# Four tiles of int8 transposes moved behind the last gate product, and two layernorm steps fused

## The chip, the cores and the metric

The kernel runs on one core of a Trainium2 chip. A core has five engines with queues of their own: TensorE (PE: matrix products and transposes, results into PSUM), VectorE (DVE), ScalarE (ACT), GpSimd (POOL) and SyncE (SP, which only issues DMAs here). The weight loads of TensorE are shown apart as PEld. The metric is the device time of one execution in microseconds; lower is better. The kernel before took 1231.49 us, the median of three runs (1229.37 to 1232.19).

## The reference, cut to what matters

One input of 625 nodes by 1024 features goes through four residual layers, each on a layernorm of what came before:

```python
x = x + gated_rgcn(_layernorm(x))     # 8 relations, then tanh(u) * z + x * (1 - z), z = [u, x] @ w_gate
x = x + int8_linear(_layernorm(x))    # one scale for the whole tensor
x = x + gcn(_layernorm(x))            # x @ W.T + b, then a sum over neighbours with symmetric norms
x = x + moe(_layernorm(x))            # top-2 of 8 experts, and a shared expert

def _layernorm(x, axis=-1, eps=1e-05):
    m = jnp.mean(x, axis=axis, keepdims=True)
    v = jnp.var(x, axis=axis, keepdims=True)
    return (x - m) / jnp.sqrt(v + eps)

# int8_linear
x_scale = jnp.maximum(jnp.abs(x2).max() / 127.0, EPS)
x_int8 = jnp.clip(jnp.round(x2 / x_scale), -128, 127).astype(jnp.int8)
acc_i32 = jax.lax.dot_general(x_int8, weight_int8.T, ..., preferred_element_type=jnp.int32)
out = acc_i32.astype(jnp.float32) * x_scale * weight_scale.T + bias
```

What matters here is the step from the first layer to the second. The int8 scale is one number for all 625 rows, so no element can be quantised before the last row has been gated and normalised.

## The kernel before, in words

The 625 nodes are five tiles of 125 rows (`NT` is 5, `P` is 125). A tile `X[t]` holds rows on partitions and 1024 features along them. TensorE contracts over partitions, so an operand that is multiplied by a weight is first transposed into `xT`, which holds eight blocks of 128 features by 625 nodes.

The first layer's relation products (L429, L649) fill the kernel up to about 836 us. Then comes the stage that the change touches:

- `gate(t, h)` (L772) multiplies `xT` of tile `t` by half `h` of the gate weights: eight products of 512 columns (sixteen records in the profile, since each is run as two). VectorE then finishes the gate with three steps on 512 columns (L785 to L787) and so completes half of `X[t]`.
- After both halves of a tile, `layernorm` (L172) normalises `X[t]` into `th[t]`, and L841 takes the largest magnitude of each row into a column of `am`.
- `transposed` (L177) turns `th[t]` back into `xT`. It works in two groups of four transposes. Each group fills one PSUM buffer of `ps_tr`, which has two, and ScalarE copies the buffer into `xT` (L186). A third group therefore waits for the first group's copy.
- `btot` holds the adjacency counts of all relations, five rows of blocks. Its transpose `aT` is made at L855 from five transposes for each row of blocks, in two PSUM buffers of the same pool (four blocks in one, the fifth in the other), and copied by ScalarE at L858. It is used only much later, at L959.
- `am1` (L863) is the largest magnitude of each partition. TensorE spreads it over all partitions (the product named amT, L865), and VectorE makes the scale and its inverse (L867 to L870).
- `quantize(t)` (L880) scales, rounds and clips `xT` of one tile in three VectorE steps into `qT`. Tile 0 is done in two halves. `quantized(t)` (L903) multiplies it by the int8 weights, held in bf16 (L908, sixteen products for a tile), and VectorE adds the result to `X[t]` and normalises it again. `columns(t)` (L925) transposes that and multiplies by the weights of the third layer (L931). The order of the two is written out at L948.

`layernorm` calls `ln_stats` (L156), which takes mean and variance, and `rsqrt` (L144): ScalarE takes the square root, VectorE the reciprocal, and one Newton step refines it. It is called with one value for a row (125x1) by every layernorm, and with five (125x5) once, for the degrees. Twenty layernorms run: five at the start, five after the gates, five after the int8 products, five after the third layer.

Three things set the order of the instructions. `on_pe` and `tc.issue_after(pe_last.ins)` chain steps on TensorE: a step may not be issued ahead of the one before it in the chain. `behind` does the same between two single instructions. Within those bounds the framework's planner orders each engine's queue by its own estimates when the kernel is built. The queue is then fixed, and each engine runs its own in that order. The adjacency transposes and tile 4's transposes (L850 to L859) are issued after `pe_last`, but `pe_last` is not advanced by them: only the amT product (L865) becomes the next `pe_last`.

## Time and profile before

| | |
|---|---|
| median of three runs | 1231.49 us |
| profiled execution, its own time | 1231.8 us |
| its span | 1230.0 us |
| mean granted TensorE clock | 0.987 |
| TensorE busy | 1192.4 us, 97% |
| VectorE busy | 846.7 us, 69% |
| ScalarE busy | 172.2 us, 14% |
| relation products (L429) on the chain | 48% |
| gate products (L777) on the chain | 6% |
| int8 products (L908) on the chain | 18 us (1.5%) |

The profile gives start and duration of each instruction, and in brackets the engine's idle time before it with what ended it. The chain of waits follows the work that ended last back through what released each step. A line such as "PE mm L908 x48" is 48 records of line 908 on TensorE. A stretch gives each engine's busy time between two moments, then the clock granted to TensorE (1.00 is full), the share of DMA that was busy and the GB/s moved.

### The profile page before, as it was taken

What the parts mean: (1) busy time and instruction counts of PE and PEld (TensorE: products, weight loads), DVE (VectorE), ACT (ScalarE), POOL (GpSimd) and SP (SyncE); (2) the same over time, 40 slices, a digit from 0 to 9 for tenths busy, and PEclk for the clock granted to TensorE, in tenths of its full rate; (3) what the DMA queues carried; (4) which work ended last, traced back from release to release, by engine and by line L of the source; (5) the groups of instructions that cost most, each with busy time, mean ns of one, the idle gap of its engine ahead of it and who ended that gap; (6) DMA issues with size and microseconds to landing.
All of it is one profiled execution on the core that took longest, in us unless ns stands there. A gap on an engine that the chain in (4) does not pass through costs nothing.

```text
span 1230.0 us, 11161 instructions
## 1 busy us (share of the span) xinstructions
PE 1192.4 (97%) x3850; PEld 653.6 (53%) x3850; DVE 846.7 (69%) x1360; ACT 172.2 (14%) x308; POOL 487.2 (40%) x227
## 2 busy tenths in 40 slices
PE   5999999999999999999999999999999999999996
PEld 2444444444444444444437888885445447766663
DVE  6879888888888888883336888865979516471111
ACT  1100000000000000000021212213321111213331
POOL 1005787888787888987700000003310000023322
PEclk9999999999999999999999999999999999999998
DMA  9995836373737373626175679606340016279973
GB/s 265 268 255 129 211 64 202 62 203 62 203 63 202 65 201 65 180 43 180 1 182 143 176 185 270 174 1 161 102 137 17 17 35 200 82 236 264 281 159 55
DMA packets 155984, 178.36 MB, mean 145 GB/s; under 512 B 78469, under 2 KB 95228, under 8 KB 155920
## 3 DMA queue, kind: packets, MB, share of 16 engines
q1 hardware_dynamic: 66082, 132.28, 37.0%
q0 software_dynamic: 72992, 13.31, 10.7%
q10 hardware_dynamic: 16846, 31.98, 8.5%
q8 instruction: 32, 0.52, 0.2%
q14 instruction: 32, 0.26, 0.1%
HBM read 131.66 MB, written 45.50 MB: 144 GB/s over the span
## 4 chain that ended last, share of the span: by engine, by line
PE 91%; DMA 4%; ACT 2%; DVE 1%; issue 1%; POOL 0%; SPq 0%; ACTq 0%; POOLq 0%; DVEq 0%
PE mm L429 48%; PE mm L649 14%; PE mm L777 6%; PE mm L931 6%; PE mm L1357 4%; PE mm L1330 3%; PE mm L959 2%; DMA w<-in_L_gnn_weight_dram 2%; PE tr L183 2%; PE mm L1259 2%; PE mm L908 1%; PE mm L1045 1%; DMA y<-yd 1%; PE lgT L1032 1%; ACT xT L186 1%
## 5 line engine op out<-in xcount | busy, mean ns | idle before, releaser
L387 POOL DMA_INDIRECT table<-hits,idx x165 | 408.1, 2474 | 198.7 <-DVE idx L383 99.3
L429 PE MATMUL mm<-w,xT 128*125 128x512 f32 x800 | 350.8, 593 | 0.2 <-DMA w<-in_L_gnn_weight_dram 0.2
L363 DVE SCALAR_TENSOR_TENSOR junk<-kr,key,wm 125x1375 f32<-125x1375 f32 x165 | 271.7, 1646 | 1.1
L429 PEld LDWEIGHTS mm<-w,xT 128*125 128x125 f32 x800 | 150.1, 188 | 192.3 <-issue 188.6
L649 PE MATMUL mm<-y,b 125*125 125x512 f32 x400 | 160.7, 402 | 2.3 <-issue 1.4
L649 PE MATMUL mm<-hi,b 125*125 125x512 f32 x400 | 159.1, 398 | 0.0
L429 PE MATMUL mm<-t,btot 128*125 128x512 f32 x320 | 143.8, 592 | 0.0
L1314 POOL DMA_INDIRECT th<-tokens,token_i x16 | 17.4, 1086 | 214.5 <-DVE token_i L1198 174.4
L429 PEld LDWEIGHTS mm<-t,btot 128*125 128x125 f32 x320 | 60.1, 188 | 77.3 <-issue 77.3
L981 POOL IOTA io<- 125x40 f32 x1 | 0.2, 207 | 227.8 <-ACT th L762 227.8
L649 PEld LDWEIGHTS mm<-y,b 125*125 125x125 f32 x400 | 75.0, 187 | 23.6 <-DVE y L614 3.4
L712 DVE SCALAR_TENSOR_TENSOR X<-mm,rc,X 125x512 f32<-125x512 f32 x80 | 60.0, 751 | 38.8 <-PE mm L649 38.0
L649 PEld LDWEIGHTS mm<-hi,b 125*125 125x125 f32 x400 | 75.1, 188 | 18.2
L429 PE MATMUL mm<-t,xT 128*125 128x512 f32 x160 | 71.9, 592 | 0.0
L429 PE MATMUL mm<-w,btot 128*125 128x512 f32 x160 | 71.9, 592 | 0.0
L931 PE MATMUL mm<-w,xT 128*125 128x512 f32 x160 | 70.0, 595 | 1.6 <-ACT xT L186 1.6
L777 PE MATMUL mm<-w,xT 128*125 128x512 f32 x160 | 71.0, 604 | 0.0
L609 ACT CAST hi<-y 125x512 fp32r<-125x512 f32 x80 | 43.3, 617 | 148.3 <-PE mm L649 131.3
L1357 PE MATMUL mm<-w,th 128*98 128x512 f32 x128 | 56.3, 592 | 0.0
L614 DVE TENSOR_TENSOR y<-y,hi 125x512 fp32r<-125x512 f32 x80 | 53.6, 681 | 0.0
L448 ACT COPY y<-mm 125x512 f32<-125x512 f32 x18 | 10.5, 586 | 302.5 <-PE mm L429 291.7
L422 DVE TENSOR_TENSOR t<-w,t 128x2048 f32<-128x2048 f32 x20 | 45.8, 2290 | 8.1 <-DMA w<-in_L_gnn_weight_dram 7.6
(220 smaller groups left out, 1170.4 us busy)
## 6 DMA issues: line engine op xcount, KB each, us to landing
w<-in_L_gnn_weight_dram SPq DMA_DIRECT2D x32, 1024.0 KB
w<-in_L_ffn_w_dram SPq DMA_DIRECT2D x16, 1024.0 KB
yd<-y ACTq DMA_DIRECT2D x70, 224.0 KB
y<-yd SPq DMA_DIRECT2D x70, 224.0 KB
table<-zero SPq DMA_DIRECT2D x4, 3054.0 KB
b<-table SPq DMA_DIRECT2D x8, 1367.2 KB
kr<-key_rows ACTq DMA_DIRECT2D x15, 601.6 KB
w<-in_L_gnn_w_gate_dram SPq DMA_DIRECT2D x8, 1024.0 KB
```

The source lines that it names most:

```text
L363: d = nc.vector.scalar_tensor_tensor(junk, kr, key[:, c : c + 1], wm[:, (EG - 1 - j) * P : (2 * EG - 1 - j) * P], op0=ALU.is_equal, op1=AL ...
L387: d = nc.gpsimd.indirect_dma_start(out=table, out_offset=bass.IndirectOffsetOnAxis(ap=idx[:, c : c + 1], axis=0), in_=hits[:, c : c + 1], ...
L422: d = nc.vector.tensor_sub(o, v, w)
L429: last = nc.tensor.matmul(ps[:P, :], lhs[:, k], rhs[:, k], start=(start and k == 0), stop=(stop and k == 3))
L609: upper.append(nc.scalar.copy(hi, y))
L614: turns.append(nc.vector.tensor_sub(lo, y, hi.bitcast(F32)))
L649: last = nc.tensor.matmul(ps[:P, :], counted[r][:, k, t * P : (t + 1) * P], part, start=(k == ks[0] and part is parts[r, h, k][0]), stop=( ...
L712: nc.vector.scalar_tensor_tensor(X[at][:, hs], v[:P, :], rc[:, r, at : at + 1], X[at][:, hs], op0=ALU.mult, op1=ALU.add,)
L777: last = nc.tensor.matmul(ps[:P, :], xT[:, 4 * i + k, t * P : (t + 1) * P], gate_w[h][i][:, k, :], start=(i == 0 and k == 0), stop=(i == 1 ...
L931: last = nc.tensor.matmul(ps[:P, :], xT[:, k, t * P : (t + 1) * P], gcn_w[h][k // 4][:, k % 4, :], start=(k == 0), stop=(k == KD - 1),)
L1330: last = nc.tensor.matmul(ps[:, :CAP], weights[e][0][:, k, f * 128 : (f + 1) * 128], tiles["xeT"][e % 2][:, k, :], start=(k == 0), stop=(k ...
L1357: last = nc.tensor.matmul(ps[:CP, :], he[:, f, j * CP : (j + 1) * CP], weights[e][1][:, f, hs], start=(f == 0), stop=(f == 1),)
```

## The change

Two things are changed.

First, the int8 transposes. Before, tile 0's transposes stood between the two gate halves of tile 3, and tile 1's between those of tile 4; those of tiles 2 and 3 stood behind the last gate product. Now those of tiles 0 to 3 all stand behind the last gate product, one tile after the other. Tile 4's stay where they were in the text, after the adjacency rows.

Second, the layernorm. For one value a row, two multiplications of the Newton step become one instruction that multiplies twice; the shape with five values keeps the two. The copy of the mean now stands behind the addition of epsilon to the variance instead of ahead of it.

```diff
@@ rsqrt
         t = small.tile(shape, F32, tag="rq_t", name="rq_t")
-        nc.vector.tensor_mul(t, v, y0)
-        nc.vector.tensor_mul(t, t, y0)
+        if shape[1] == 1:
+            nc.vector.scalar_tensor_tensor(t, v, y0, y0, op0=ALU.mult, op1=ALU.mult)
+        else:
+            nc.vector.tensor_mul(t, v, y0)
+            nc.vector.tensor_mul(t, t, y0)
         nc.vector.tensor_scalar(t, t, -0.5, 1.5, op0=ALU.mult, op1=ALU.add)
@@ ln_stats
         nc.vector.bn_aggr(mv, st.rearrange("p a b -> p (a b)"))
-        nc.vector.tensor_copy(mean_rstd[:, 0:1], mv[:, 0:1])
         ve = small.tile([P, 1], F32, tag="ln_ve", name="ln_ve")
         nc.vector.tensor_scalar_add(ve, mv[:, 1:2], EPS)
+        nc.vector.tensor_copy(mean_rstd[:, 0:1], mv[:, 0:1])
         rsqrt(mean_rstd[:, 1:2], ve, [P, 1])
@@ the gate loop
             with tc.issue_after(pe_last.ins):
                 pe_last, added = gate(t, h)
-            if h == 0 and t >= 3:
-                on_pe(transposed, xT, (t - 3) * P, th[t - 3], P)
             if t > 0:
@@ behind the gate loop
-    for t in (NT - 3, NT - 2):
+    for t in range(NT - 1):
         on_pe(transposed, xT, t * P, th[t], P)
```

## The prediction

> **What bounds the kernel now.** I read the page first, for the bound; then the chain in order of time around the changed steps; then TensorE's timeline there, VectorE's timeline, and stretches of one clock state each.

> ```profile
> PE 1192.4 (97%) x3850; PEld 653.6 (53%) x3850; DVE 846.7 (69%) x1360; ACT 172.2 (14%) x308; POOL 487.2 (40%) x227
> PEclk9999999999999999999999999999999999999998
> PE 91%; DMA 4%; ACT 2%; DVE 1%; issue 1%; POOL 0%; SPq 0%; ACTq 0%; POOLq 0%; DVEq 0%
> ```

> TensorE is the bound, busy 97% and 91% of the chain, so a step counts only if it moves TensorE's next dense product. The chain shows where TensorE is not dense:

> ```profile
> 907.47 6.87 PE mm L777 x16
> 914.34 0.44 PE tr L183 x4
> 914.80 0.59 ACT xT L186
> 915.44 0.66 PE tr L183 x4
> ...
> 924.50 1.93 PE tr L183 x8
> 926.43 11.11 PE mm L908 x48
> 937.53 0.44 PE tr L183 x4
> ```

> Last gate product, then twelve microseconds in which each transpose waits for ScalarE's copy out of PSUM, then the int8 products (L908). TensorE's timeline there:

> ```profile
> 916.75 0.85 PE L855 MATMUL tr<-ident,btot 125*125 125x125 f32 x5 [0.19 <-ACT xT L186]
> 918.12 0.81 PE L855 MATMUL tr<-ident,btot 125*125 125x125 f32 x5 [0.51 <-ACT aT L858]
> 920.85 1.32 PE L855 MATMUL tr<-ident,btot 125*125 125x125 f32 x5 [0.56 <-ACT aT L858]
> 922.62 1.41 PE L855 MATMUL tr<-ident,btot 125*125 125x125 f32 x5 [0.25 <-ACT aT L858]
> 926.22 11.31 PE L908 MATMUL mm<-w,btot 128*125 128x512 bf16 x48
> ```

> A row of the adjacency matrix (five transposes) takes 1.36 us, later 1.8 us. The stretches say why (second PE share, granted clock before the DMA share):

> ```profile
> 914.17:917.58 3.41, 2.98 (x22) 2.28 (x20) 3.03 (x6) 2.21 (x5) 0.00 (x0) 1.00 0.97 302
> 917.58:920.99 3.41, 1.78 (x12) 1.38 (x12) 2.74 (x9) 2.22 (x7) 0.00 (x0) 1.00 0.38 147
> 920.99:924.40 3.41, 2.80 (x11) 2.12 (x11) 2.21 (x9) 1.27 (x4) 0.00 (x0) 0.50 0.00 0
> 924.40:927.82 3.42, 3.32 (x12) 2.65 (x13) 3.28 (x7) 1.37 (x4) 0.00 (x0) 0.50 0.02 5
> ```

> The granted clock is halved from 920.99 to 927.82, into the first products. VectorE meanwhile:

> ```profile
> 914.38 0.69 DVE L785 TENSOR_TENSOR z<-mm,gx 125x512 f32<-125x512 f32 x1 [4.05 <-PE mm L777]
> 918.39 0.16 DVE L151 TENSOR_TENSOR rq_t<-ln_ve,rq_y 125x1 f32<-125x1 f32 x1
> 918.59 0.16 DVE L152 TENSOR_TENSOR rq_t<-rq_t,rq_y 125x1 f32<-125x1 f32 x1
> 924.09 0.29 DVE L886 TENSOR_SCALAR btot<-btot 128x500 bf16<-128x500 bf16 x1
> 925.26 0.29 DVE L886 TENSOR_SCALAR btot<-btot 128x500 bf16<-128x500 bf16 x1
> ```

> It idles 4.05 us until the last gate product is out; the first half of the first int8 tile is then ready at 924.38, the second at 925.55. TensorE came to L908 only at 926.22: its own queue was last, by 0.67 us behind even the second half.

> **Part 1, the gates lose two tiles of transposes.** Between gate products, eight transposes took 891.75 to 892.60 and 906.45 to 907.31: 0.85 and 0.86 us, 0.107 each. Both go: -1.71. The last gate product ends at 914.17 - 1.71 = 912.46. VectorE's idle time of 4.05 us covers its own backlog, so all of it reaches VectorE.

> **Part 2, they stand behind the last gate.** A tile there took 1.27 and 1.31 us (914.17, 915.44, 916.75): ScalarE's copy sets the pace. Four tiles take 4 x 1.29 = 5.16, to 917.62, where before the adjacency rows began at 916.75. Alone this would cost 0.87 us.

> **Part 3, the planner's new order.** Compared as built, TensorE's queue changes more than the diff says. Before: all five adjacency rows and tile 4's transposes stand ahead of the first int8 product. After: four tiles, two rows, the small product that spreads the maximum (amT), two rows, three int8 products, the fifth row, three products, tile 4's eight transposes, then the other 42. Rows at 1.36: 917.62, 918.98, 920.34, 921.70; TensorE is free at 921.70 + 5 x 0.107 = 922.24. The thirteen later transposes cost 13 x 0.107 = 1.39 among products instead of a pace set by ScalarE. Their PSUM buffers: the fourth row's copy ends near 921.70 + 1.3 = 923.0, and the fifth row is reached at 923.25; tile 4's first group waits about 0.1. That wait would hold the products queued behind it. No DMA moves: SP's and POOL's queues are the same, and ScalarE has one square root placed between the fifth and sixth copies (0.20 us at most).

> **Part 4, the layernorm steps.** The fused instruction replaces two that stand 0.20 apart. No row has this form at 125x1; its neighbours take 0.14 to 0.17, so it saves between 0.0 (if it cost two) and 0.2; I take 0.20, since the same kind of operand, two scalars per row, costs the apply step no extra gap (0.04 us, like its neighbours). The copy of the mean now follows the step it delayed: -0.08 (917.52, 917.60). On the chain to int8 that is 0.28 once. Twenty layernorms run. The first tiles' saving at 23 us, 0 to 0.28, is behind the weight load that TensorE awaits until 82.11, with DMA shares of 0.82 to 1.10 from 60 to 82 us: I take 0. The fifteen others lie beside products. The nearest to the path is tile 0's after the int8 product: ready at 936.41 for a transpose at 937.37. After, I get its second half's product at 927.44, VectorE free of two tiles' quantising at 927.85, ready at 933.3 for about 934.3: still 1 us of cover, beyond which each late microsecond would show.

> **The sum.** VectorE has the first half ready at 924.38 - 1.71 - 0.28 = 922.39, the second at 923.56. With some 0.2 us to reach TensorE, products begin at 922.6 (TensorE free 922.24). Sixteen at full clock took 3.45 us (952.81 to 956.26), so 48 take 10.35; with 1.39 of transposes they end at 934.34, against 937.37: -3.03. The product at 937.37 is followed by dense work, so the shift should pass through to the end. The profiled execution took 1231.8 us (span 1230.0 and 1.8 around it): 1231.8 - 3.0 = 1228.8. It lies 0.3 above the median, 1231.49; the three runs span 2.8.

> **Rival 1: the clock is lost all the same (0.29).** It fell after a window with TensorE busy 1.78 of 3.41 us, not after 2.98. The change shortens the sparse stretch from 916.75-924.5 to 917.62-922.24, so a window of 3.41 us need not fall inside it. The drops at 641.1, 842.5, 920.99, 1081.4 and 1105.3 (from the granted clock of 1 us stretches) lie whole multiples of 3.41 us apart, so where a window falls against this stretch is chance. If it is halved again from 920.99 to 927.82: the fourth row ends at 922.77, products begin at 922.8, 5.02 us at half do 2.51 of the 11.74 us of work, end 937.05: -0.3, 1231.5. One window only: end 935.34, -2.0, 1229.8. [...]

> **Rival 2, slower: the clock falls inside the four tiles (0.15).** If a stretch of nothing but transposes counts as idle, the drop comes from 3.4 us after 912.46, at 915.9. Rows and tiles then go at 1.8 instead of 1.36: 1.3 tiles and four rows each lose 0.45, 2.4 in all; the fourth row ends near 925.1, products begin at 925.2, and the clock rises only after a full window of them, 3.4 to 6.8 us on, which costs 1.7 to 3.4. End 938.6 to 940.3: +1.3 to +3.0, 1233.1 to 1234.8. It decides from a drop before 917.6. Against it: 914.17 to 917.58 held transposes alone, and the clock stayed 1.00. [...]

> **How the numbers follow.** The forecast (0.56) is that the clock holds: 1228.8, its own range 1227.8 to 1229.6. 0.2%, 2.5 us, is about what a measurement of this kernel can tell from no change: faster means under 1229.0, which takes four fifths of the forecast, 0.45. Slower, over 1234.0, is most of rival 2 and unknown waits: 0.12. The rest, 0.43, lies between. The range, 1227.6 to 1232.6, reaches over rival 1 and leaves out most of rival 2 and a little below.

> **What would show it.** Gate products without a break from 899.7 but for 0.1 us; TensorE's four tiles at 1.29 us each; the first L908 about 3.6 us earlier; thirteen transposes among L908 without waits on ScalarE; the granted clock 1.00 throughout. It is wrong if the 0.50 stretch stays as long, if L908's first six products wait for VectorE, or if tile 0's layernorm comes after TensorE.

## The result, and the profile after

The changed kernel took 1228.11 us, the median of 15 runs (1224.68 to 1232.79), against 1231.23 us for the kernel before, the median of 15 runs on the same chip (1228.68 to 1232.96). The ratio is 0.9976 with a 95% interval of 0.9967 to 0.9986: 3.1 us less, at the edge of what a measurement of this kernel can tell. The profiled execution took 1228.25 us, with a span of 1226.4 us and a mean granted clock of 0.991 (0.987 before).

The page of the kernel after, in the order of the first lines shown of before: busy time, granted clock by slices, the chain by engine.

```profile
PE 1190.8 (97%) x3850; PEld 652.5 (53%) x3850; DVE 844.5 (69%) x1340; ACT 172.4 (14%) x308; POOL 490.2 (40%) x227
PEclk9999999999999999999999999999999999999998
PE 93%; DMA 2%; ACT 2%; DVE 1%; issue 1%; POOL 0%; SPq 0%; POOLq 0%; DVEq 0%; ACTq 0%
```

TensorE is still the bound. VectorE has 20 instructions fewer, one for each layernorm. The stage itself, TensorE's timeline of the kernel after (start, duration, then in brackets the idle time before it and what ended it):

```profile
912.19 1.02 PE L186 MATMUL tr<-ident,th 125*128 125x125 f32 x8
913.45 1.13 PE L186 MATMUL tr<-ident,th 125*128 125x125 f32 x8 [0.24 <-ACT xT L189]
...
917.39 0.94 PE L856 MATMUL tr<-ident,btot 125*125 125x125 f32 x5
...
921.50 0.81 PE L856 MATMUL tr<-ident,btot 125*125 125x125 f32 x5 [0.56 <-ACT aT L859]
922.14 0.81 PE L909 MATMUL mm<-w,btot 128*125 128x512 bf16 x3
922.86 0.81 PE L856 MATMUL tr<-ident,btot 125*125 125x125 f32 x5
923.51 0.81 PE L909 MATMUL mm<-w,btot 128*125 128x512 bf16 x3
924.23 1.07 PE L186 MATMUL tr<-ident,th 125*128 125x125 f32 x8
925.14 9.23 PE L909 MATMUL mm<-w,btot 128*125 128x512 bf16 x42
934.20 1.02 PE L186 MATMUL tr<-ident,th 125*128 125x125 f32 x8
```

Four tiles stand behind the last gate product, then four rows at 1.37 us. The first int8 product (L909, before L908) comes directly behind the fourth row; the thirteen remaining transposes stand between products without a wait. From the gates' end to the next transposes it is 22.01 us (912.19 to 934.20), where before it was 23.20 (914.17 to 937.37).

Stretches of 3.41 us of the kernel after, cut on the grid on which its clock drops lie (at 643.90, 841.87 and 1097.87 us, 58 and 75 steps of 3.413 us apart; first the length, then TensorE's busy time; the granted clock stands ahead of the DMA share):

```profile
913.52:916.94 3.42, 3.05 (x23) 2.29 (x24) 2.77 (x10) 2.75 (x7) 0.00 (x0) 1.00 0.84 304
916.94:920.35 3.41, 2.44 (x17) 1.72 (x16) 2.78 (x7) 2.46 (x6) 0.00 (x0) 1.00 0.00 0
920.35:923.76 3.41, 2.85 (x20) 2.13 (x20) 3.06 (x9) 1.65 (x5) 0.00 (x0) 1.00 0.00 0
923.76:927.18 3.42, 3.42 (x21) 2.33 (x20) 3.31 (x6) 1.64 (x4) 0.00 (x0) 1.00 0.02 5
```

The clock stays full. The sparsest stretch has TensorE busy for 2.44 us; before, the one that lost the clock had 1.78. VectorE's timeline of the kernel after:

```profile
912.39 0.69 DVE L788 TENSOR_TENSOR z<-mm,gx 125x512 f32<-125x512 f32 x1 [2.60 <-PE mm L780]
916.36 0.22 DVE L152 SCALAR_TENSOR_TENSOR rq_t<-ln_ve,rq_y 125x1 f32<-125x1 f32 x1
916.61 0.15 DVE L156 TENSOR_SCALAR rq_t<-rq_t 125x1 f32<-125x1 f32 x1
921.39 0.29 DVE L887 TENSOR_SCALAR btot<-btot 128x500 bf16<-128x500 bf16 x1
922.63 0.29 DVE L887 TENSOR_SCALAR btot<-btot 128x500 bf16<-128x500 bf16 x1
```

The first half of the first int8 tile is ready at 921.68, 0.46 us before TensorE comes to it.

Where the 3.55 us between the two profiled executions (1231.8 and 1228.25) lie, from the same events in both traces:

| stretch | before | after | difference |
|---|---|---|---|
| start to first gate product | 841.98 | 841.71 | -0.27 |
| gates, to the end of the last gate product | 72.19 | 70.48 | -1.71 |
| from there to the first product of the third layer | 24.83 | 23.45 | -1.38 |
| the rest of the span | 291.00 | 290.76 | -0.24 |
| around the span | 1.8 | 1.85 | +0.05 |

The change touches the second and third rows: -3.09. The other rows lie outside it; the clock drops there too, at other moments in each execution (643.9 to 647.3 after and 641.1 to 647.9 before, for one).

### The profile page after: what moved, and what is told of

Same layout as the page of the kernel before. It is cut to its first block, busy times and chain, and to the rows that moved or that the text cites. A ratio compares the mean times of both kernels' runs of the same rounds, so it can differ in the third digit from the quotient of the medians.

```text
span 1226.4 us, 11142 instructions
## 1 busy us (share of the span) xinstructions
PE 1190.8 (97%) x3850; PEld 652.5 (53%) x3850; DVE 844.5 (69%) x1340; ACT 172.4 (14%) x308; POOL 490.2 (40%) x227
## 4 chain that ended last, share of the span: by engine, by line
PE 93%; DMA 2%; ACT 2%; DVE 1%; issue 1%; POOL 0%; SPq 0%; POOLq 0%; DVEq 0%; ACTq 0%
PE mm L432 50%; PE mm L652 14%; PE mm L780 6%; PE mm L932 6%; PE mm L1358 4%; PE mm L1331 3%; PE mm L960 2%; PE tr L186 2%; PE mm L1046 1%; PE mm L909 1%; PE mm L1260 1%; DMA y<-yd 1%; PE lgT L1033 1%; ACT xT L189 1%; DMA X<-in_x_dram 1%
## 5 line engine op out<-in xcount | busy, mean ns | idle before, releaser
L432 PEld LDWEIGHTS mm<-w,xT 128*125 128x125 f32 x800 | 151.1, 189 | 192.9 <-issue 190.3
L780 PEld LDWEIGHTS mm<-w,xT 128*125 128x125 f32 x160 | 30.4, 191 | 39.0 <-issue 38.6
```

What stands on the lines that cost most here:

```text
L432: last = nc.tensor.matmul(ps[:P, :], lhs[:, k], rhs[:, k], start=(start and k == 0), stop=(stop and k == 3))
L780: last = nc.tensor.matmul(ps[:P, :], xT[:, 4 * i + k, t * P : (t + 1) * P], gate_w[h][i][:, k, :], start=(i == 0 and k == 0), stop=(i == 1 ...
```

## The experiments

Theory 1 is that of the prediction: the gates give 1.71, and the rest comes from the clock that holds, because the sparse stretch is shorter. The rivals: the planner's order alone gives the rest and the clock is a bystander; or the layernorm steps do. Experiments marked as adding work repeat or add products and transposes whose results nothing uses or that are written again with the same values. "The stage" is the third row of the table.

**The transposes moved, the layernorm as before.**

```diff
-        if shape[1] == 1:
-            nc.vector.scalar_tensor_tensor(t, v, y0, y0, op0=ALU.mult, op1=ALU.mult)
-        else:
-            nc.vector.tensor_mul(t, v, y0)
-            nc.vector.tensor_mul(t, t, y0)
+        nc.vector.tensor_mul(t, v, y0)
+        nc.vector.tensor_mul(t, t, y0)
...
+        nc.vector.tensor_copy(mean_rstd[:, 0:1], mv[:, 0:1])
         nc.vector.tensor_scalar_add(ve, mv[:, 1:2], EPS)
-        nc.vector.tensor_copy(mean_rstd[:, 0:1], mv[:, 0:1])
```

> The four tiles stand behind the last gate product as in the changed kernel, the layernorm is the one of before. Theory 1 (nearly all of the gain is the two tiles that leave the gates and the planner's new order): the first int8 product comes no later than 0.3 us after that of the changed kernel, since there TensorE's fourth adjacency row ended 0.46 us behind VectorE; about 1228.3 us, 2.9 under before. Theory 2 (the shorter layernorm is what lets the int8 products begin early): half of the gain or more is lost, 1229.7 us or above.

Measured: 1227.88 us (median of 5), ratio 0.9965 (0.9952 to 0.9978). The planner makes the same mix of rows and products, and the first int8 product stands 9.95 us behind the gates' end, just as in the kernel after. The move alone has the whole gain, as far as the intervals can tell; the fused step isn't needed for it.

**The layernorm alone.** The kernel before with the two layernorm edits of the change.

> Only the layernorm is changed, the transposes stand as before. Theory 1: in the kernel before, TensorE came to the first int8 product 0.67 us after VectorE had even the second half ready, and the fifteen other layernorms lie beside products, so 1231.0 to 1231.2 us, no change. Theory 2: the twenty layernorms give 0.15 to 0.28 us each on the path, up to 3 us: 1229.5 us or below.

Measured: 1231.53 us (median of 11), ratio 0.9993 (0.9983 to 1.0003): no change that can be told. In its profile the clock is lost in the stage, for one window. Stretches on the grid of its own drops:

```profile
917.21:920.62 3.41, 2.22 (x15) 1.65 (x14) 2.71 (x10) 1.95 (x7) 0.00 (x0) 1.00 0.56 216
920.62:924.03 3.41, 1.96 (x13) 1.54 (x14) 2.69 (x9) 2.04 (x6) 0.00 (x0) 1.00 0.00 0
924.03:927.45 3.42, 3.42 (x13) 2.46 (x12) 3.28 (x7) 1.16 (x2) 0.00 (x0) 0.50 0.02 5
```

The stretch with 2.22 us of TensorE busy keeps the clock, the one with 1.96 loses it. Its stage took 23.78 us, where the kernel before took 24.83: the transposes stand as before, but the clock was halved for one window here and for two there. So the third row of the table depends on where the windows fell in the two executions compared.

**The change without the planner's mix.** The first int8 product is held back until tile 4's transposes are out, as before.

```diff
-        transposed(xT, (NT - 1) * P, th[NT - 1], P)
+        turned = transposed(xT, (NT - 1) * P, th[NT - 1], P)
...
+                if t == 0 and h == 0 and k == 0:
+                    behind(last, turned)
```

> As the changed kernel, but the first int8 product is held behind the fifth adjacency row and tile 4's transposes, as they stood before. Theory 1 (the planner's new order carries part of the gain): rows at 1.36 us and tile 4 at 1.0 us put the first int8 product near 925.3 us where the changed kernel has 922.1, less the 1.4 us of transposes that are then done: 1.7 us lost with the clock at 1.00, 3 to 4 us if the longer sparse stretch (917.4 to 925.3) halves the clock, which it should in most runs. 1230 to 1231.5 us. Theory 3 (only the gates' shorter time counts): 1228.1 us, as the changed kernel.

Measured: 1231.68 us (median of 11), ratio 0.9994 (0.9985 to 1.0003): the gain is gone. In the profiled execution (1229.66 us) the clock held; its gates took 70.48 like those of the kernel after, and its stage 24.57 instead of 23.45, so the order alone is worth 1.12 us. The median lost more than that, and the granted clocks go with it: the three with a mean clock of 0.991 or more took 1229.0 to 1229.9, the other eight, at 0.988 to 0.990, 1231.3 to 1232.6. Another execution of the same kernel, profiled, tells whether the stage is where the clock goes.

> The changed kernel with the old order ahead of the int8 products (e3) once more: its first profile took 1229.7 us and kept the full clock in this stage, its median is 1231.7. If the clock makes the difference, a run at 1231 us or above shows the clock at 0.50 for 3.4 to 6.8 us behind the last gate product, and 26 to 27 us from there to the third layer's products (24.6 with the clock kept). If such a run keeps the clock there, the difference lies elsewhere.

That execution took 1230.22 us, not the 1231 or above that was looked for. It lost the clock there, for one window, and its stage took 25.82 us. Stretches on each one's grid, first of the first profile, then of the second:

```profile
918.44:921.85 3.41, 2.44 (x17) 1.72 (x16) 2.78 (x7) 2.35 (x6) 0.00 (x0) 1.00 0.01 2
921.85:925.27 3.42, 2.09 (x15) 1.53 (x13) 3.10 (x8) 1.76 (x5) 0.00 (x0) 1.00 0.00 0
925.27:928.68 3.41, 3.06 (x18) 2.27 (x19) 2.89 (x6) 1.52 (x4) 0.00 (x0) 1.00 0.02 5
```

```profile
915.65:919.06 3.41, 2.81 (x19) 1.96 (x17) 2.76 (x7) 2.39 (x6) 0.00 (x0) 1.00 0.13 50
919.06:922.47 3.41, 1.91 (x12) 1.53 (x13) 3.10 (x10) 1.98 (x6) 0.00 (x0) 1.00 0.00 0
922.47:925.89 3.42, 2.96 (x14) 2.54 (x14) 3.21 (x6) 1.44 (x4) 0.00 (x0) 0.50 0.02 5
```

The same instructions, cut at another place: with 2.09 us busy in the sparsest window the clock holds, with 1.91 it falls. So the planner's mix does two things: it takes 1.12 us out of the queue, and it fills the windows so that few places of the cut are left that lose the clock. Slide a window of 3.41 us along TensorE's timeline in steps of 0.1 us, and let the bound lie between 1.96 us, the most that lost the clock in this stage, and 2.09, the least that kept it. In the kernel after, the sparsest window has 1.97 us busy, and between none and 0.5 of the 3.4 us of possible starts lie under the bound; without the mix it goes down to 1.73, and 1.0 to 2.1 of the 3.4 us lie under it. That doesn't account for all: neither profiled execution reaches the median of 1231.68, which lies 3.8 us above that of the move alone on the same chip. The order (1.12) and one lost window (25.82 less 24.57, 1.25) make 2.4 of it; where the rest was lost isn't shown.

**The mix alone, forced into the kernel before.** The fifth row behind the third product, tile 4's transposes behind the sixth; tiles 0 and 1 stay between the gates.

```diff
-        for k in range(NT):
+        for k in range(NT - 1):
+            row(k)
...
-        transposed(xT, (NT - 1) * P, th[NT - 1], P)
...
+                if t == 0 and h == 0 and k in (3, 6):
+                    behind(d, last)
+                last = d
+                if t == 0 and h == 0 and k in (2, 5):
+                    with tc.issue_after(d.ins):
+                        last = row(NT - 1) if k == 2 else transposed(xT, (NT - 1) * P, th[NT - 1], P)
```

> The kernel before, with its transposes between the gate products and its layernorm, but the fifth adjacency row stands behind the third int8 product and tile 4's transposes behind the sixth. Theory 1 (the order alone gives little, because VectorE then ends last): the first int8 product can begin at 924.4 to 924.6 us instead of 926.2 and carries 1.4 us of transposes more, so 0.3 us gained at the same clock, up to 1.5 if the clock recovers earlier: 1230 to 1231 us. Theory 4 (the order is the whole gain, the place of the two tiles is none): 1228.5 us.

Measured: 1235.15 us (median of 12), ratio 1.0027 (1.0016 to 1.0038): slower, where some 1230 to 1231 was expected. TensorE's timeline of this kernel:

```profile
921.08 1.14 PE L854 MATMUL tr<-ident,btot 125*125 125x125 f32 x5 [0.56 <-ACT aT L857]
922.02 0.41 PE L868 MATMUL amT<-ident,am 125*128 125x125 f32 x1
924.49 1.54 PE L911 MATMUL mm<-w,btot 128*125 128x512 bf16 x3 [2.06 <-DVE btot L889]
925.83 1.25 PE L854 MATMUL tr<-ident,btot 125*125 125x125 f32 x5
```

With two tiles fewer behind the gates, TensorE is through its four rows before VectorE has quantised, and stands still for 2.06 us; and the clock is halved from 921.4 to 928.2. The drop comes ahead of the standstill, behind a window with 1.95 us busy. Another profiled execution of it shows whether that is usual.

> The order alone (e4) once more, for a second profile: its first one took 1233.3 us, its median is 1235.2. If the clock is what costs it 3 us, a run near the median shows TensorE at 0.50 for 10 us or more between the last gate product and the first products of the third layer's weights, or a second halved stretch right behind, and the time from the last gate product to those is 26 us or more (25.3 in the first profile, 24.8 before). If the clock is no cause, that time stays near 25.3 and the loss lies elsewhere.

The clock was lost there again (922.1 to 928.9), behind a window with 1.90 us busy. But that execution took 1233.29 us, again well under the median, and its stage 25.26, near the 25.34 of the first and only some 0.5 us above the 24.83 of the kernel before. By the terms set beforehand, the 3.2 us that the median lost against before lie in the main outside what these two profiles show of the stage; where they lie stays open. To part the two causes, the same order was run with work added: two unused products behind each of the four rows and eight behind amT.

```diff
+            filler = fill(2, row(k, filler))
...
+    behind(pe_last, filler)
+    pe_last = fill(8, pe_last)
```

> The run with the planner's order alone (e4, 3.2 us slower than before), with two unused products behind each of its four rows and eight behind the small product that spreads the maximum, where TensorE stood still for 2.06 us. Clock theory (the order alone was slow because the longer wait halves the clock for longer): 1230 to 1231 us, under before. Rival (something else in that order costs the 3 us): 1234 us or above, as without the products.

Measured: 1231.24 us (median of 12), ratio 0.9994 (0.9982 to 1.0006), mean clock 0.9902 over its runs against 0.9857 without the added products. Work that nobody uses made this kernel 3.9 us faster; the two medians are from two chips, but the ratios to the kernel before, each on its own chip, lie apart beyond their intervals. TensorE comes to the first int8 product some 10.1 us behind the gates' end in either (914.41 to 924.49 and 916.63 to 926.72), so it isn't the time until VectorE is ready that was won; what differs in the stage is the clock, full here and halved there. The stage took 23.77 us against 25.34 and 25.26, so 1.5 of the 3.9 us are seen in it. The rest isn't placed: this profiled execution took 1233.46 us, 2.2 above its median and no less than those without the products.

**Twelve tiles instead of four** (added work: each of the four is transposed three times).

```diff
-    for t in range(NT - 1):
+    for t in range(3 * (NT - 1)):
+        t = t % (NT - 1)
         on_pe(transposed, xT, t * P, th[t], P)
```

> The changed kernel with the transposes of the first four tiles done three times over behind the last gate product (the result is the same, 8 tiles of transposes are added). Theory 1 (tiles at 1.29 us keep TensorE busy enough for the full clock): the clock stays at 1.00 through 15.5 us of them, 8 x 1.29 = 10.3 us more, 1238.5 us. Rival (transposes count as idle): the clock is halved at the latest 6.8 us into them, tiles then take 1.8 us, 3 to 5 us on top: 1242 us or above.

Measured: 1239.46 us (one execution). Stretches on its grid:

```profile
921.06:924.48 3.42, 3.09 (x22) 2.08 (x20) 0.18 (x2) 2.72 (x6) 0.00 (x0) 1.00 0.02 5
924.48:927.89 3.41, 2.92 (x21) 2.06 (x20) 0.48 (x1) 2.94 (x6) 0.00 (x0) 1.00 0.00 0
```

For 16 us TensorE did nothing but transposes (and the one amT product), 1.27 to 1.37 us a tile, and the clock stayed full throughout (1.00 in these two stretches, with 3.09 and 2.92 us busy). This takes away rival 2 of the prediction: these fp32 transposes alone kept the clock.

**The first four rows three times** (added work).

```diff
-        for k in range(NT):
+        for k in (*range(NT - 1), *range(NT - 1), *range(NT)):
```

> The changed kernel with the transposes of the first four adjacency rows done three times over (8 rows are added, the result is the same). Theory 1 (rows, with 0.54 us of transposes in 1.36 us, are too sparse for the full clock): it is halved 3.4 to 6.8 us into them, rows then take 1.8 us, and the first int8 products run at half clock: 8 x 1.36 = 10.9 us more, and 3 to 6 on top, 1242 to 1245 us. Rival (the clock was lost before for another reason than the rows' spacing): clock 1.00, 1239 us.

Measured: 1241.86 us (one execution). Stretches on its grid:

```profile
917.43:920.84 3.41, 2.51 (x16) 2.00 (x16) 2.79 (x7) 2.03 (x5) 0.00 (x0) 1.00 0.00 0
920.84:924.26 3.42, 1.78 (x12) 1.24 (x10) 0.12 (x1) 2.03 (x6) 0.00 (x0) 1.00 0.00 0
924.26:927.67 3.41, 2.81 (x10) 2.25 (x10) 0.00 (x0) 1.04 (x5) 0.00 (x0) 0.50 0.02 5
```

Rows, unlike tiles, lose the clock: the first window that holds rows alone has 1.78 us busy, and the clock is halved at its end, until 937.9. A row at half clock takes 1.93 us instead of 1.37. So it is how densely these transposes stand that counts here, not that they are transposes: five of them in 1.37 us (1.78 us busy of 3.41) were too few, eight in 1.27 to 1.37 us (2.92 and 3.09 busy) were enough.

**The clock kept in the kernel before** (added work: two unused products of 512 columns behind each of the five rows, in the time in which TensorE waits for ScalarE).

```diff
+            if k in (0, 1, 2, 3, 4):
+                filler = fill(2, d)
         transposed(xT, (NT - 1) * P, th[NT - 1], P)
```

> The kernel before, with two products of 512 bf16 columns behind each of the five adjacency rows, into a PSUM tile that nobody reads; at full clock they take 0.43 us and fit into the 0.8 us in which TensorE awaits ScalarE. Clock theory (most of the change's gain is that the clock is no longer halved in this stage): the clock stays at 1.00 from 916 to 928, rows keep 1.36 us, the products after them lose nothing: 1.5 to 2.4 us under before. Queue theory (the gain is the shorter queue of TensorE alone): the time stays that of before, within 0.5 us.

Measured: 1232.04 us (median of 12), ratio 1.0004 (0.9988 to 1.0021): no gain. In the stage it did what it should: the clock stayed full, and the first int8 product came 10.32 us behind the gates' end (915.46 to 925.78), 1.73 earlier than in the kernel before. What became of it, on TensorE and then by stretches on its grid:

```profile
925.78 10.53 PE L927 MATMUL mm<-w,btot 128*125 128x512 bf16 x48
936.79 1.04 PE L183 MATMUL tr<-ident,th 125*128 125x125 f32 x8 [0.48 <-DVE th L168]
939.23 10.94 PE L950 MATMUL mm<-w,xT 128*125 128x512 f32 x21 [1.40 <-ACT xT L186]
```

```profile
935.81:939.22 3.41, 1.54 (x11) 0.90 (x10) 3.32 (x6) 1.06 (x2) 0.00 (x0) 1.00 0.00 0
939.22:942.63 3.41, 3.40 (x4) 1.46 (x5) 3.34 (x8) 0.00 (x0) 0.00 (x0) 0.50 0.00 0
```

In this execution the products were through before tile 0's layernorm was. TensorE waited 0.48 us for it and 1.40 us for the copy behind, and in that hole the window had 1.54 us busy: the clock that was saved in the stage fell 15 us later, and the work from the first product of the third layer to the MoE stage took 140.62 us instead of 138.87. Of the 2.51 us by which the products ended sooner behind the gates (20.85 instead of 23.36), the stage kept 1.06, and the next stretch took 1.75 back. This is one way in which the gain is lost, and a likely one: by the same sliding window as above, 1.3 to 2.6 of the 3.4 us of starts put that hole under the bound. It isn't the whole account of the median, since the execution took 1234.93 us, 2.9 above it, and the 12 runs spread from 1228.95 to 1237.18.

**The clock filled in the kernel after** (added work: two unused products behind each of the four rows).

```diff
+            if k in (0, 1, 2, 3):
+                filler = fill(2, d)
```

> The changed kernel, with the same two products behind each of the four rows that stand ahead of the int8 products. Clock theory: in the changed kernel the clock holds in this stage in most runs, so 0 to 0.8 us under the changed kernel, about 0.28% under before, and fewer runs above 1230 us. Rival (the products get in the way of the rows): 0.5 to 1 us above the changed kernel.

Measured: 1230.1 us (median of 12), ratio 0.9983 (0.9968 to 0.9999). Its stage took 23.94 us in the profile, against 23.45, and six of the 12 runs lie above 1230 us where three of 15 of the changed kernel did, so the rival fits better than the clock theory. There was hardly any clock left to save there (1.00 through the stage in the kernel after), and the added products push the planner's order about: one int8 product ahead of the fifth row instead of three.

**A step outside the change.** TensorE also waits just ahead of the first gate product, for a copy of ScalarE that stands behind tanh. In the kernel after:

```profile
838.13 1.02 PE L680 MATMUL tr<-ident,X 125*128 125x125 f32 x8
841.23 0.65 PE L680 MATMUL tr<-ident,X 125*128 125x125 f32 x4 [2.09 <-ACT xT L681]
```

The experiment has the changed kernel's tanh wait until the last of those copies is issued.

```diff
-        nc.scalar.activation(th[t], X[t], AF.Tanh)
+        behind(nc.scalar.activation(th[t], X[t], AF.Tanh), turned_u[-1])
```

> The changed kernel, with the first layer's tanh on ScalarE held behind the last copies of transposed sums into xT, for which TensorE waits 2.1 us at 839 us before the gates. It tests the clock at another place: the halved clock at 842 to 846 us follows that wait. Clock theory: the wait goes (2 us) and with it the halved stretch (3.4 us at half, 1.7 us): 2 to 3.7 us under the changed kernel, 1224.5 to 1226 us. Rival (the halved clock there has another cause): 1226 us at best, with the clock still at 0.50 for 3.4 us. The gates could then overtake VectorE, which awaits the reload of X: no gain.

Measured: 1226.4 us (median of 6, 1224.85 to 1228.64) against 1232.03 for the kernel before, ratio 0.995 (0.9932 to 0.9968). Its profile has the wait down to 0.24 us:

```profile
838.55 1.02 PE L682 MATMUL tr<-ident,X 125*128 125x125 f32 x8
839.81 0.65 PE L682 MATMUL tr<-ident,X 125*128 125x125 f32 x4 [0.24 <-ACT xT L683]
```

The gates begin at 840.29 and take 68.98 us instead of 70.48, with the clock full from their start (in the kernel after it was halved from 841.8 to 845.3). One execution can't show that the wait was the cause: of the 13 others profiled, all with the wait, four kept the clock there too. But with the wait the thinnest window of 3.41 us has 1.32 us busy, and without it 3.17. The profiled execution itself took 1228.64 us, no less than that of the kernel after (1228.25), with 3.3 us more behind the start of the MoE stage, where its clock was halved for longer (1074.46 to 1081.29 and 1098.35 to 1105.18, against 1097.87 to 1104.70 in the kernel after). By its median the kernel with the later tanh beats the kernel before clearly; against the changed kernel's 0.9976 (0.9967 to 0.9986), from another chip, the two intervals just touch.

## Why the prediction was right

It said 1228.8 us, in a range from 1227.6 to 1232.6; the median was 1228.11 and the profiled execution 1228.25.

- **Part 1, the gates.** 1.71 forecast, 1.71 measured (72.19 to 70.48). Where the clock was full at the gates' start it is 1.72 (70.50 in the run with the layernorm alone, 68.78 in that with the move alone). The absolute end, 912.19 and not 912.46, has the 0.27 us that this execution was ahead when the gates began.
- **Part 2, four tiles.** 5.16 forecast, 5.20 measured (912.19 to 917.39). What two more tiles behind the gates cost alone was put at 0.87; between the stage of the kernel before with the clock kept (23.77) and that of the change without the mix and with the clock kept (24.57) it is 0.80, though the first of these also carries a layernorm wait.
- **Part 3, the order.** The queue ran as forecast. From the gates' end it was to be 10.14 us to the first int8 product and 21.88 to the next transposes; it was 9.95 and 22.01. The thirteen transposes among the products were put at 0.107 each, 1.39 in all, but the stretch from the first product to the next transposes took 12.06 instead of 11.74: each change between products and transposes costs some 0.05 to 0.11 us more (three products take 0.72 where 0.65 was reckoned, five transposes 0.65 where 0.54 was, eight 0.91 where 0.86 was).
- **Part 4, the layernorm.** It was to bring 0.28 us on the way from the last gate product to the scale, with 0.20 from the fused step and 0.08 from the copy. From VectorE's first gate step to the end of the reduction `am1` it brought 0.18 (7.05 to 6.87): the fused instruction takes 0.22 us and not 0.16, so its step of 0.25 replaces two of 0.39 and saves 0.14; the copy saves 0.05. VectorE won another 0.54 that the prediction didn't have: amT stood behind a row at half clock in TensorE's queue, and VectorE idled 0.99 us for it; after, 0.46.
- **What comes last.** This step failed. The forecast had VectorE as the later of the two, at 922.39, with 0.2 us on top, the author's estimate, which the kernel after does not show. TensorE was later: its fourth row was out at 922.14, VectorE's first half at 921.68. The half microsecond of amT is why. So the fused step could bring nothing here, which the run without it shows.
- **The clock.** Forecast as held, with 0.29 for its loss. It held in the changed kernel's profile, and in the two others with the same order (the move alone, the later tanh). The reason given, a shorter sparse stretch, is right as far as it goes. What is behind it is the measure: with 1.54 to 1.96 us busy in a window of the grid the clock fell in all seven cases in this stage and the stretch behind it, and with 2.09 or more it held. The seven: 1.54 (the filler in the kernel before), 1.78 (the kernel before, and the first four rows three times), 1.90 and 1.95 (the mix alone, twice), 1.91 (without the mix, second profile) and 1.96 (the layernorm alone); it held with 2.09 (without the mix, first profile), 2.22 (the layernorm alone) and 2.44 (the kernel after). Rival 1's "chance" is where the grid cuts the stretch, and the changed order leaves it little.
- **The sum.** -3.03 forecast, -3.09 over gates and stage. It didn't part clock from order, and the experiments do: of the stage's -1.38, the clock kept brings -1.06 (the kernel before with filler), two more tiles cost 0.80, the mix brings -1.12. These three are differences between profiles of single executions, which add up because each run stands in two of them; the first includes the layernorm wait that its filler uncovered. That the sum fits to 0.06 us is in part luck: it was worked out from an execution that lost the clock in the stage for two windows. Against the 23.78 us of the run with the layernorm alone, which lost one, the change's stage is 0.33 us shorter and not 1.38.
- **Cover of tile 0's layernorm.** Put at 1 us, "beyond which each late microsecond would show". It was 1.15 (ready at 933.05, reached at 934.20), and the filler in the kernel before shows what is behind it: 0.48 us of wait on the layernorm, and the clock.
- **Rival 2** fell with the twelve tiles: 16 us of transposes at a clock of 1.00. Its return of the clock "only after a full window" of products was the author's estimate, from halved stretches of 3.41 and 6.83 us; in the kernel before the clock was full again at 927.81, 1.6 us after the first of the products (926.22).

## What to carry to other kernels

In this kernel a stretch of waiting cost more than its waits: behind rows with waits of 0.51 to 0.56 us TensorE ran at 0.50 for 6.83 us (920.98 to 927.81 in the kernel before). Look at the busy share in windows of the length that the drops keep (3.41 us here), and move dense work into the thinnest one before shortening a dependency elsewhere. A move that takes work out of a dense stage paid at once here (1.71 us in the gates), but it paid in full only where something else stood in the wait that it moved to: the order in which int8 products went between the late transposes decided whether the gain was there at all (ratio 0.9965 for the move alone, with that order, and 0.9994 for the change without it). And when a stage gets shorter, read how much cover the next stage's input has, since here it was there that the filler's gain was given back (1.75 of 2.51 us in its profile).
